# A graph layer on one core: squares turned on VectorE, sums sent through DRAM, products one group later

## The chip, the cores and the metric

The kernel runs on one core of a Trainium2 chip. The metric is the device time of one execution in microseconds (us). Before the change it is 2057.62 us, the median of three runs (2055.93 to 2058.0).

The core has a matrix engine (TensorE, in the profile PE; its loads of the stationary operand are PEld), VectorE (DVE), ScalarE (ACT), GpSimd (POOL) and SyncE (SP). Sixteen DMA engines move data between DRAM and the on-chip memories. Here POOL issues the indirect DMAs (gathers of rows by a list of indices) and SP the plain ones.

## The reference

`x` is 6250 x 512 (f32), `src` and `dst` are the ends of 100000 edges, sorted by `dst`. A graph convolution is applied twice, around a layer norm:

```
norm = -dinv[src] * dinv[dst]                    # dinv from the out-degrees
prop(h) = segment_sum(h[src] * norm, dst)        # for each node the sum of its neighbours' rows
conv(h; W0, W1, b) = h @ W0 + prop(h) @ W1 + b
h   = relu(layernorm(x))
h   = leaky(layernorm(conv(h; W1_0, W1_1, b1)) * gamma + beta)
out = x + conv(h; W2_0, W2_1, b2)
```

## The kernel before, in words

A prologue (up to some 110 us) makes the layer norm of x, the degrees, and a table in DRAM (`tab[0]`, rows of 512 values and one more for dinv). Then `usual_path` runs two layers with the same loop.

**Gathers and groups.** The edges lie in 782 chunks of 128. For each chunk POOL gathers the 128 source rows into one of 55 places in a ring (`gather_to`, line 444). Three chunks make a unit, which spans at most 32 target nodes, and four units a group: 66 groups a layer, 12 chunks in each but the first. `choose(g)` (VectorE) makes the 0/1 matrices `sel` of a group from the sorted targets, in layer 0 `scale` multiplies them by the gathered rows' dinv, and `sums(g)` (line 615) multiplies `sel` with the gathered rows: 24 matmul rows in the profile (two for each f32 matmul), four strips of 32 partitions. ACT takes the result out of PSUM to `agg[g]` (line 625). A place is free for a later gather when its matmul is done.

**Blocks.** The nodes lie in 49 blocks of 128 (46 whole ones on the usual way and three in `EARLY`, 46 to 48, which are handled partly ahead of time). A block's targets lie in two or three groups (`inside[i]`). When the last of them is summed, `turn` loads the block after next (`load`, `AHEAD` = 2), turns the block's own rows `h` with four TensorE transposes into `hT` (`own`, line 519, and an ACT eviction, line 521), and `place` moves the sums from their unit order to their nodes with one matmul a group (line 645, by the 0/1 matrices `there` of `spots`). ACT scales the result to `an` (line 698). `first_half` turns `an` with four transposes (line 705), VectorE copies them to `aT` (line 707), and the four products `hT @ W0` run. `second` adds the four products `aT @ W1` (all line 531) and calls `finish`: in layer 0 bias, layer norm, leaky relu, and two row stores, to the table of layer 1 (`tab[1]`, line 679) and to `h_tab` (line 684); in layer 1 bias, x (`load_x`) and the store of the output.

**Order.** TensorE, POOL and SP run in the order in which the program issues; VectorE and ACT are put in order by a scheduler that goes by its own cost model. An engine that waits holds up what stands behind it in its own queue. In the loop over groups, `turn` of a block stands before the group's `sums`, `first_half` behind them, and `second` before the following group's `place`, or with the next block's own turn. From the last 12 groups on (`JOIN`) `dense` runs both halves together behind the sums. At the end of layer 0 `gather_ahead` starts 18 chunks of layer 1 from the rows stored so far (those of blocks up to 46), and the rest wait for the stores of blocks 47 and 48. At the start SP loads h of blocks 0 and 1, and then the biases (`load_rest(4)`), which `widen` spreads over the partitions after the second group's sums; `look_up` scales the first raw chunks.

Of the kernel before, what the change touches and what calls it, by code (L numbers as in the profile page):

```python
# [8 lines left out]
F32 = mybir.dt.float32  # L9
# [10 lines left out]
P = 128  # L20
# [4 lines left out]
Q = 32  # L25
NQ = P // Q
# [7 lines left out]
JOIN = 12  # L34
# [8 lines left out]
def gnn_kernel(  # L43
# [61 lines left out]
    h_tab = dram.tile([N, D], F32, name="h_tab")  # L105

# [10 lines left out]
    first = const.tile([P, NQ * NS + 1], F32, name="first")  # L117
# [76 lines left out]
    def load_rest(k):  # L194
# [55 lines left out]
    with tc.tile_pool(name="turn", bufs=1) as wp, tc.tile_pool(  # L250
# [11 lines left out]
        nc.vector.tensor_copy(first, first_ps)  # L262
# [145 lines left out]
def usual_path(tc, have):  # L408
    nc = tc.nc
    (x, out, tab, h_tab, ndinv, sidx, dlx, iota_r, w_sb, W2_1, W2_0, w_late, ident, eps, ones, first, nodes_ps, node_of, minus,  # L410
     unsorted, dinv, sdinv, bias1, bias2, gam, bet, unseen, unit, N, E, D, NB, NC, NU, NS, KD, rows, places, R,
     load_rest, sc, pick, src_lo, src_hi, eidx, e_src, zero_row, p_id) = (
        have[n] for n in ("x out tab h_tab ndinv sidx dlx iota_r w_sb W2_1 W2_0 w_late ident eps ones first nodes_ps node_of "
# [13 lines left out]
    with ExitStack() as es:  # L427
# [5 lines left out]
        own_h, own_x, agg, placed, started, pre, late, theres = {}, {}, {}, {}, {}, {}, {}, {}  # L433
# [48 lines left out]
        def look_up(tag):  # L482
# [13 lines left out]
            both = pool.tile([P, D], F32, name="an")[:, : 8 * NB].rearrange("p (j k b) -> p j k b", j=4, k=2)  # L496
# [12 lines left out]

        def load(layer, i):  # L510
            if i not in EARLY:
                load_h(layer, i, "h", AHEAD)

        def own(layer, i):

            h, r = own_h.pop(i), rows[i]
            ps = psum.tile([P, KD, P], F32, name="hT_ps")
            for kc in range(KD):
                nc.tensor.transpose(ps[:, kc, :r], h[:r, kc * P : (kc + 1) * P], ident[:r, :r])  # L519
# [54 lines left out]
        def count_late(sel, chunk):  # L574
# [5 lines left out]
            for q in some:  # L580
                for b in range(LATE):
                    for k, t in enumerate(chunk[q]):
                        hot = pool.tile([P, P], F32, name="there", bufs=3)
# [4 lines left out]
            cnt = pool.tile([P, LATE, P], F32, name="cnt", bufs=1)  # L588
# [19 lines left out]
        def sums(layer, g, sel, chunk, cnt=None, of=(0, NQ)):  # L608
# [14 lines left out]
            if of[1] >= n:  # L623
                agg[g] = pool.tile([P, D], F32, name="agg", bufs=3)
                nc.scalar.activation(agg[g][: n * Q], ps[: n * Q], AF.Copy)  # L625

        def spots(i, some):

            r = rows[i]
            there = [pool.tile([P, P], F32, name="there", bufs=3) for _ in some]  # L630
            for t, g in zip(there, some):
                m = Q * (unit[g + 1] - unit[g])
                behind[1] = nc.vector.tensor_scalar(t[:m, :r], iota_r[:m, :r], node_of[:m, g : g + 1],  # L633
# [3 lines left out]
        def place(i, some):  # L637

            r = rows[i]
            if i not in placed:  # L640
                placed[i] = psum.tile([P, D], F32, name="an_ps", bufs=1)
            there = theres.pop(i) if i in theres else spots(i, some)
            for t, g in zip(there, some):
                m = Q * (unit[g + 1] - unit[g])
                nc.tensor.matmul(placed[i][:r], t[:m, :r], agg[g][:m, :], start=(g == inside[i][0]),  # L645
                                 stop=(g == inside[i][-1]))

# [38 lines left out]
        def turn(layer, i, left=()):  # L686

            r = rows[i]
# [4 lines left out]
            hT = None if i in EARLY else own(layer, i)  # L693
# [3 lines left out]
            an = pool.tile([P, D], F32, name="an")  # L697
            nc.scalar.activation(an[:r], placed.pop(i)[:r], AF.Copy, scale=ndinv[:r, i : i + 1])  # L698
            return hT, an

        def first_half(layer, i, hT, an, between=None):
            r = rows[i]
            ps = psum.tile([P, KD, P], F32, name="hT_ps")
# [4 lines left out]
            if between is not None:  # L708
                between()
            if i not in EARLY:  # L710
                started[i] = psum.tile([P, D], F32, name="u_ps")
                products(started[i], hT, w_late[:, 1] if layer else w_sb[1], rows[i], True, False)
            return aT

        def second(layer, i, aT):
            w1 = w_late[:, 0] if layer else w_sb[0]
# [4 lines left out]

        def dense(layer, i, hT, an, between=None):
            second(layer, i, first_half(layer, i, hT, an, between))

        def check():
# [19 lines left out]
            of = pool.tile([P, D], F32, name="xt")[0:1, :]  # L745
            nc.vector.tensor_sub(of[:, :NU], first[0:1, 1 : NU + 1], first[0:1, :NU])
# [49 lines left out]
        for layer in range(2):  # L796
# [4 lines left out]
            i, chosen, left = 0, {}, []  # L801
            for g in range(NS):
                gather_to(layer, STEP * unit[g] + R)
                if layer == 0 and g == NS // 2:
                    for k, w in enumerate((W2_1, W2_0)):
                        nc.sync.dma_start(w_late[:, k], w.rearrange("(k p) d -> p k d", p=P))
# [4 lines left out]
                due = []  # L811
                if g == NS - JOIN or inside[i].stop > g:
                    for k, aT in left:
                        second(layer, k, aT)
                    left = []
                while inside[i].stop <= g:
                    due.append((i, turn(layer, i, left)))
                    left = []
                    i += 1
                if g == NS - 2:  # L820
                    for k, (hT, an) in due:
                        dense(layer, k, hT, an)
# [4 lines left out]
                sel, chunk = chosen.pop(g) if g in chosen else choose(g)  # L827
                of = (NQ // 2, NQ) if g == NS - 1 else (0, NQ)
                if layer == 0 and g < NS - 1:
# [4 lines left out]
                if g < NS - 1:  # L834
                    chosen[g + 1] = choose(g + 1)
# [375 lines left out]
```

## Time and profile before

| what | us |
|---|---|
| median of three runs | 2057.62 |
| profiled execution, its own time | 2057.13 |
| its span | 2055.2 |
| PE busy | 1686.4 |
| POOL busy | 1513.0 |
| DVE busy | 701.1 |
| ACT busy | 406.6 |
| gathers in q0 | 415.98 MB, 67.5% of the DMA engines' time |
| plain DMAs in q1 | 110.12 MB, 14.8% |
| TensorE's mean granted clock | 0.912 |

Busy time of PE overlaps and its ends are modelled. A row of the profile's fifth part names line, engine, operation, output and input, shape and count; behind the bar stand the busy time, the mean of one in ns, and the idle time of the engine just before such instructions, with what ended most of it. "issue" there is time for which the profile shows no wait. A row of the order of time has start, length, engine, line, operation, count, and in brackets the idle time before it and what ended it. A row of the stretches has its bounds, its length, busy time and count by engine, the clock, the share of the DMA engines and GB/s.

### The profile page before, as it was taken

The page shows a single profiled execution, that of the slowest core. Times are in us where ns is not written, and L with a number is a line of the kernel's source. Part 1 is how long each engine was busy: PE and PEld are TensorE (multiplying, and loading weights), DVE is VectorE, ACT ScalarE, POOL GpSimd, SP SyncE. Part 2 cuts the span into 40 slices and gives each one's busy share as a digit, 9 for nine tenths or more (in the row PEclk, how much of TensorE's full clock was granted, in tenths as well). Part 3 has the DMA queues.
Part 4 walks back from the last instruction along what each step waited for, and adds up shares of the span by engine and source line. Part 5 has one row for each costly group of instructions (what it writes and reads, how often), then busy time and mean ns, then how long its engine had stood idle before and what let it go on. Part 6 is the DMA issues. An engine that isn't in the chain of part 4 may idle for free.

```text
span 2055.2 us, 19878 instructions
## 1 busy us (share of the span) xinstructions
PE 1686.4 (82%) x6814; PEld 675.0 (33%) x6814; DVE 701.1 (34%) x1501; ACT 406.6 (20%) x740; POOL 1513.0 (74%) x1578
## 2 busy tenths in 40 slices
PE   5569997788777778777899888888888888898987
PEld 4444432233222223333333223233322223333332
DVE  7955442334434333543452211122121212121221
ACT  8766221112211111221120100110110111010110
POOL 5757777777777777777767777777777777777774
PEclk9769998899898889889999989999999999999999
DMA  9978888888898888888877887887788888778875
GB/s 360 360 258 237 274 265 255 247 262 263 255 298 249 255 248 263 262 254 255 256 240 236 253 249 245 251 255 246 247 252 250 246 252 255 243 249 255 270 237 158
DMA packets 189415, 527.47 MB, mean 257 GB/s; under 512 B 34550, under 2 KB 36112, under 8 KB 189304
## 3 DMA queue, kind: packets, MB, share of 16 engines
q0 software_dynamic: 125120, 415.98, 67.5%
q1 hardware_dynamic: 64184, 110.12, 14.8%
q8 instruction: 56, 0.92, 0.2%
q14 instruction: 55, 0.45, 0.1%
HBM read 474.31 MB, written 51.66 MB: 256 GB/s over the span
## 4 chain that ended last, share of the span: by engine, by line
PE 47%; DMA 25%; POOL 11%; issue 9%; DVE 5%; ACT 1%; SPq 1%; DVEq 0%; POOLq 0%; ACTq 0%
DMA places<-tab,sidx 19%; PE u_ps L531 19%; PE ps L615 13%; POOL places L444 11%; PE an_ps L645 9%; DMA places<-tab,lidx 5%; PE hT_ps L519 2%; PE hT_ps L705 2%; DVE lo L340 1%; DVE hi L340 1%; SPq L508 1%; PE hT_ps L491 1%; PE hT_ps L586 0%; DVE sel L604 0%; DVE st L665 0%
## 5 line engine op out<-in xcount | busy, mean ns | idle before, releaser
L444 POOL DMA_INDIRECT places<-tab,sidx x1212 | 1148.8, 948 | 386.5 <-issue 271.3
L615 PE MATMUL ps<-places,sel 128*32 128x512 f32 x3128 | 523.6, 680 | 155.8 <-DMA places<-tab,sidx 90.2
L645 PE MATMUL an_ps<-agg,there 128*128 128x512 f32 (+1 forms) x580 | 284.5, 623 | 101.8 <-ACT agg L625 96.8
L444 POOL DMA_INDIRECT places<-tab,lidx x270 | 255.5, 946 | 82.2 <-issue 62.1
L615 PEld LDWEIGHTS ps<-places,sel 128*32 128x32 f32 x3128 | 105.0, 119 | 542.7 <-issue 195.9
L570 DVE TENSOR_TENSOR sel<-dlx,nodes_ps 128x384 f32<-128x384 f32 (+3 forms) x134 | 72.2, 540 | 423.8 <-PE ps L615 423.4
L625 ACT ACTIVATE agg<-ps 128x512 f32<-128x512 f32 (+1 forms) x132 | 78.3, 594 | 573.1 <-PE ps L615 552.7
L531 PE MATMUL u_ps<-w,hT 128*128 128x512 f32 (+1 forms) x392 | 178.5, 599 | 13.0 <-ACT hT L521 13.0
L645 PEld LDWEIGHTS an_ps<-agg,there 128*128 128x128 f32 (+1 forms) x580 | 110.6, 200 | 228.8 <-ACT agg L625 115.0
L531 PE MATMUL u_ps<-places,hT 128*128 128x512 f32 (+1 forms) x392 | 179.1, 600 | 2.2 <-ACT hT L521 2.2
L531 PE MATMUL u_ps<-w,aT 128*128 128x512 f32 (+1 forms) x392 | 176.9, 594 | 1.7 <-DVE aT L707 1.7
L531 PE MATMUL u_ps<-places,aT 128*128 128x512 f32 (+1 forms) x392 | 176.6, 593 | 1.5 <-DVE aT L707 1.5
L604 DVE TENSOR_TENSOR sel<-sel,places 128x384 f32<-128x384 f32 (+11 forms) x73 | 35.1, 484 | 375.5 <-DMA places<-tab,sidx 370.0
L656 DVE TENSOR_TENSOR u_ps<-u_ps,bias 128x512 f32<-128x512 f32 x46 | 32.2, 699 | 288.5 <-PE u_ps L531 288.5
L521 ACT ACTIVATE hT<-hT_ps 128x512 f32<-128x512 f32 (+1 forms) x98 | 58.2, 594 | 284.3 <-PE hT_ps L519 283.7
L633 DVE TENSOR_SCALAR there<-iota_r,node_of 128x128 f32<-128x128 f32 (+1 forms) x290 | 86.9, 303 | 66.4 <-PE an_ps L645 63.5
L698 ACT ACTIVATE an<-an_ps,ndinv 128x512 f32<-128x512 f32 (+1 forms) x98 | 67.1, 684 | 206.7 <-PE an_ps L645 206.5
L236 POOL DMA_INDIRECT places<-in_x_dram,sidx x55 | 79.1, 1438 | 36.8 <-issue 9.1
L668 ACT ACTIVATE sd<-mv,eps 128x1 f32<-128x1 f32 (+1 forms) x49 | 14.4, 294 | 455.4 <-DVE mv L666 455.4
L531 PEld LDWEIGHTS u_ps<-w,aT 128*128 128x128 f32 (+1 forms) x392 | 71.8, 190 | 84.3 <-issue 78.3
L531 PEld LDWEIGHTS u_ps<-places,aT 128*128 128x128 f32 (+1 forms) x392 | 72.1, 190 | 83.1 <-issue 80.4
L531 PEld LDWEIGHTS u_ps<-w,hT 128*128 128x128 f32 (+1 forms) x392 | 71.3, 192 | 85.1 <-issue 71.5
(166 smaller groups left out, 1272.9 us busy)
## 6 DMA issues: line engine op xcount, KB each, us to landing
places<-tab,sidx POOLq DMA_INDIRECT x1212, 3.9
h_tab<-g SPq DMA_DIRECT2D x48, 256.0 KB
xt<-in_x_dram SPq DMA_DIRECT2D x48, 256.0 KB
out_dram<-t SPq DMA_DIRECT2D x48, 256.0 KB
tab<-t SPq DMA_DIRECT2D x47, 256.0 KB
h<-tab SPq DMA_DIRECT2D x46, 256.0 KB
h<-h_tab SPq DMA_DIRECT2D x46, 256.0 KB
tab<-places SPq DMA_DIRECT2D x22, 528.0 KB
```

Source lines behind the costliest of these rows:

```text
L236: nc.gpsimd.indirect_dma_start(out=places[:, t, :D], out_offset=None, in_=x, in_offset=bass.IndirectOffsetOnAxis(ap=sidx[:, t : t + 1], ax ...
L340: nc.vector.tensor_tensor(t, s[:, g * 2 * GJ : (g + 1) * 2 * GJ].rearrange("p (j s) -> p j s", s=2)[:, :, None, :] .to_broadcast([EP, GJ, ...
L444: nc.gpsimd.indirect_dma_start(out=places[:, t % R, :] if own_scale else zr(layer, t), out_offset=None, in_=x if layer == 0 and t < RAW el ...
L519: nc.tensor.transpose(ps[:, kc, :r], h[:r, kc * P : (kc + 1) * P], ident[:r, :r])
L521: nc.scalar.activation(hT[:, :, :r], ps[:, :, :r], AF.Copy)
L531: nc.tensor.matmul(u_ps[:r], hT[:, kc, :r], w[:, kc, :], start=(start and kc == 0), stop=(stop and kc == KD - 1))
L570: nc.vector.tensor_tensor(sel[:, q : q + k, :w, :], of, node[:, q : q + k, None, :].to_broadcast([P, k, w, Q]), op=OP.is_equal)
L615: nc.tensor.matmul(ps[q * Q : (q + 1) * Q, :], sel[:, q, s, :], zr(layer, chunk[q][s]), start=(s == 0), stop=(s == len(chunk[q]) - 1 and ( ...
L625: nc.scalar.activation(agg[g][: n * Q], ps[: n * Q], AF.Copy)
L633: behind[1] = nc.vector.tensor_scalar(t[:m, :r], iota_r[:m, :r], node_of[:m, g : g + 1], -(1.0 + i * P), op0=OP.subtract, op1=OP.is_equal)
L645: nc.tensor.matmul(placed[i][:r], t[:m, :r], agg[g][:m, :], start=(g == inside[i][0]), stop=(g == inside[i][-1]))
L698: nc.scalar.activation(an[:r], placed.pop(i)[:r], AF.Copy, scale=ndinv[:r, i : i + 1])
```

## The change

1. `own` no longer uses TensorE. A block of h is loaded as four strips of 32 partitions: strip c holds, for its partition i, the 128 columns from 128c on of rows i, 32+i, 64+i and 96+i (`load_squares`: four DMAs, each with 128 runs of 512 bytes). One VectorE transpose (`turn_squares`), which turns squares of 32 x 32 in place in the layout, gives `hT`, with feature 4p+k on partition p. The weights are loaded in that order of rows, `(p k) d`.
2. The scaled sums go from PSUM by ACT to `an`, from there by a DMA on ACT's queue to DRAM (`a_tab`), and are read back as squares (`sh`) by four DMAs on SP; one VectorE transpose makes `aT`. The three blocks of `EARLY` keep TensorE's transposes, with strided columns.
3. Before the last 12 groups (`FLUSH`) the order in a group is: sums(g); both products of the block that was pending; place, scaling, store, loads and turns of the block that is complete with group g-1, which is then pending. So all eight matmuls of a block run a group later, together.
4. `choose` runs one group further ahead, `scale` of the next group stands before `sums(g)`, `spots` makes its up to three matrices in one tile, ahead of the sums; `first` is copied only where the check uses it; some tiles share buffers. In the last 12 groups `turn`, sums and `dense` keep their order.

```diff
-                nc.sync.dma_start(t, w.rearrange("(k p) d -> p k d", p=P))
+                nc.sync.dma_start(t, w.rearrange("(p k) d -> p k d", p=P))
...
+        def load_squares(to, of, i):
+            for c in range(P // S):
+                nc.sync.dma_start(to[c * S : (c + 1) * S],
+                                  of[i * P : (i + 1) * P, c * P : (c + 1) * P].rearrange("(g i) f -> i g f", i=S))
+
+        def turn_squares(to, of):
+            return nc.vector.transpose(to.rearrange("p k (g i) -> p g k i", i=S), of.rearrange("p g (j k) -> p g k j", k=KD))
+
         def load(layer, i):
             if i not in EARLY:
-                load_h(layer, i, "h", AHEAD)
+                own_h[i] = pool.tile([P, P // S, P], F32, name="h", bufs=AHEAD)
+                load_squares(own_h[i], h_tab if layer else tab[0], i)
 
         def own(layer, i):
             h, r = own_h.pop(i), rows[i]
+            if i not in EARLY:
+                hT = pool.tile([P, KD, P], F32, name="hT", bufs=1)
+                turn_squares(hT, h)
+                return hT
...
-        def place(i, some):
+        def place(i, some, there=None):
...
+        def scaled_rows(i):
...
+            nc.scalar.activation(an, placed.pop(i), AF.Copy, scale=ndinv[:, i : i + 1])
+            nc.scalar.dma_start(a_tab[layer_of[0]][i * P : (i + 1) * P, :], an)
+            sh = pool.tile([P, P // S, P], F32, name="sh", bufs=1)
+            load_squares(sh, a_tab[layer_of[0]], i)
+            return sh
...
+        def turned(i, an):
+            if i not in EARLY:
+                aT = pool.tile([P, KD, P], F32, name="aT", bufs=1)
+                behind[2] = turn_squares(aT, an)
+                return aT
...
-        def first_half(layer, i, hT, an, between=None):
...
-        def second(layer, i, aT):
...
+        def dense(layer, i, hT, aT):
+            w0, w1 = (w_late[:, 1], w_late[:, 0]) if layer else (w_sb[1], w_sb[0])
             if i not in EARLY:
                 started[i] = psum.tile([P, D], F32, name="u_ps")
+                products(started[i], hT, w0, rows[i], True, False)
             whole = i not in started
             u_ps = psum.tile([P, D], F32, name="u_ps") if whole else started.pop(i)
             products(u_ps, aT, w1, rows[i], whole, True)
             finish(layer, i, u_ps)
...
-                if g == NS - JOIN or inside[i].stop > g:
-                    for k, aT in left:
-                        second(layer, k, aT)
-                    left = []
+                due, new = [], []
+                if g == NS - FLUSH:
+                    for k, hT, aT in pending:
+                        dense(layer, k, hT, aT)
+                    pending = []
                 while inside[i].stop <= g:
-                    due.append((i, turn(layer, i, left)))
-                    left = []
+                    if g >= NS - FLUSH:
+                        due.append((i, turn(layer, i)))
+                    else:
+                        new.append(i)
                     i += 1
...
-                sel, chunk = chosen.pop(g) if g in chosen else choose(g)
+                sel, chunk = chosen.pop(g)
+                if g < NS - 1:
+                    chosen[g + 1] = choose(g + 1)
+                theres = [spots(k, inside[k]) for k in new]
...
+                if layer == 0 and g < NS - FLUSH:
+                    scaled = scale(*chosen[g + 1])
                 sums(layer, g, sel, chunk, count_late(sel, chunk) if layer == 1 else None, of)
...
-                if g < NS - JOIN - 1 and inside[i].stop <= g + 1:
-                    theres[i] = spots(i, inside[i])
+                if g < NS - FLUSH:
+                    with ExitStack() as order:
+                        if layer == 0 and scaled is not None:
+                            order.enter_context(tc.issue_after(scaled.ins))
+                        for k, hT, aT in pending:
+                            dense(layer, k, hT, aT)
+                        pending = []
+                        for k, there in zip(new, theres):
+                            place(k, inside[k], there)
+                            sh = scaled_rows(k)
+                            pending.append((k, own_part(layer, k), turned(k, sh)))
                 for k, (hT, an) in due:
-                    if g < NS - JOIN:
-                        left.append((k, first_half(layer, k, hT, an)))
-                    else:
-                        dense(layer, k, hT, an)
+                    dense(layer, k, hT, turned(k, an))
```

More of the change, by code (lines that the diff above doesn't have):

```diff
@@ L105, in gnn_kernel @@
     h_tab = dram.tile([N, D], F32, name="h_tab")
+    a_tab = [dram.tile([N, D], F32, name=f"a_tab{i}") for i in range(2)]
     ident = const.tile([P, P], F32, name="ident")
@@ L432, in usual_path @@
         behind, behind_rows, summed = {}, {}, {}
-        own_h, own_x, agg, placed, started, pre, late, theres = {}, {}, {}, {}, {}, {}, {}, {}
+        layer_of = [0]
+        own_h, own_x, agg, placed, started, pre, late = {}, {}, {}, {}, {}, {}, {}
         SHIFTED = D - D % P
@@ L684, in finish, with own_part @@
                 nc.sync.dma_start(h_tab[i * P + lo : i * P + hi, :], g[lo:hi])
-        def turn(layer, i, left=()):
-            r = rows[i]
+        def own_part(layer, i):
             if layer == 1 and i not in EARLY:
@@ L800, in usual_path @@
                     load(layer, i)
[L801 removed]
+            i, chosen, pending = 0, {}, []
+            layer_of[0] = layer
             for g in range(NS):
```

95 lines of the change are left out of this document (50 added, 45 removed).

## The prediction

> **What bounds the kernel now.** I read the page first. It suggests TensorE, with 82% busy and 47% of the chain, so I checked that against POOL.
>
> ```profile
> span 2055.2 us, 19878 instructions
> PE 1686.4 (82%) x6814; PEld 675.0 (33%) x6814; DVE 701.1 (34%) x1501; ACT 406.6 (20%) x740; POOL 1513.0 (74%) x1578
> L444 POOL DMA_INDIRECT places<-tab,sidx x1212 | 1148.8, 948 | 386.5 <-issue 271.3
> q1 hardware_dynamic: 64184, 110.12, 14.8%
> ```
>
> A gather is 0.948 us busy and has some 0.30 us of "issue" before it: 1.25 us each, which the 74% does not count. The stretches of line 444 alone (length, POOL busy, clock, DMA share, GB/s) show that nothing comes between:
>
> ```profile
> 300.00:350.00 50.00, 37.93 (x40) 0.85 0.83 242
> 650.00:700.00 50.00, 37.82 (x41) 0.93 0.86 264
> 1200.00:1250.00 50.00, 37.82 (x40) 0.91 0.81 247
> 1700.00:1750.00 50.00, 37.83 (x40) 0.91 0.82 254
> ```
>
> 37.8 us is 40 gathers of 0.945, and 40 x 1.25 = 50: POOL issues without a break, in both layers. Its order of time has only these holes (start, length, idle before):
>
> ```profile
> 153.52 0.97 POOL L444 DMA_INDIRECT places<-tab,sidx  x1 [12.15 <-PE ps L615]
> 1052.23 0.94 POOL L454 DMA_INDIRECT places<-tab,eidx  x1 [5.57 <-DMA tab<-t]
> 1077.56 0.99 POOL L444 DMA_INDIRECT places<-tab,sidx  x1 [2.80 <-DMA tab<-pre]
> 2031.74 0.94 POOL L444 DMA_INDIRECT places<-tab,lidx  x1 [0.30 <-issue]
> ```
>
> From 153.5 to 2032.7 there are 1494 gathers: 1494 x 1.25 = 1867 us of the 1879; the two holes in the middle are 7.8 us beyond the usual 0.3. TensorE in this time is paced by the gathers: the list of waits has 282 us of its loads and 125 us of its matmuls in L615 waiting for places. A faster TensorE gains nothing where POOL has no hole. What can change is the start, the layer change, the tail, or the pace of the gathers itself.
>
> **The change part by part.** All is reckoned on the profiled execution, 2057.1 us (span 2055.2 and 1.9 around it); the median is 2057.6.
>
> *TensorE.* For 46 blocks in each of two layers go 4 turns of h and 4 of the sums, 0.44 + 0.59 us a block in the chain: 92 x 1.03 = 95 us. The wait for agg before place (96.8 us in all) goes too before the last 12 groups, since place now follows the next group's sums. Worth 0: POOL's 15.0 us a group (12 x 1.25) hide it. Without that cover it would be 190 us.
>
> *ACT and VectorE.* ACT loses 92 evictions hT of 0.595 (55 us), and issues 92 stores behind an; ACT is 20% busy, so 0. VectorE loses 92 copies aT of 0.687 and gains 184 turns of 128x512. No row shows such a turn. The nearest are the 128x512 f32 operations at 0.69 to 0.76; a cast of 128x896 took 0.62, so below is some 0.4, above I allow four times the copy, 2.8. I take 0.69: net +64 us on an engine 34% busy, off the path. Removing the copy first (0.43 us at 16 us) lies beside loads: 0.
>
> *The way by DRAM.* After an (0.69) ACT issues the store, SP waits for it, issues four loads, VectorE turns. Landings: the store tab<-t issued at 1049.46 released POOL at 1052.2 (2.8 us), that of tab<-pre at 1072.7 took 4.5 beside gathers, the bias loads of 130.4 to 136.4 some 5.5. I take 4.5 for each way, since gathers run beside both: 0.3 + 4.5 + four issues of 0.35 + 4.5 + 0.7 = 11.4 us, between 8.0 (2.8 each) and 13.4 (5.5 each). Products a group later hide it under sums(g+1) 2.7 and the own products 3.4, but place(k+1) stands behind the products of k on TensorE. So block to block: 0.7 + 11.4 + 3.4 + 2.6 = 18.1 us. Some 46 blocks finish in 63 groups, three in four; the fourth group adds its sums: (3 x 18.1 + 2.7) / 4 = 14.3 us a group against POOL's 15.0. It fits, with 5% to spare, and the 55 places let TensorE lag by over a group: cost 0. The Trainium skill, "DMA: Bandwidth & Descriptors", section "Anatomy of one DMA", puts some 2 us of fixed time on every DMA, most of it the write's receipt. By an estimate from it the way is 6.4 us and the loop 10.5 a group, comfortably hidden; the landings of 2.8 to 5.5 here say otherwise.
>
> *What waits behind it.* The turn of the sums waits on VectorE for its squares; behind it stand finish(k), the next spots and the choose of two groups on. sums(g+1) needs none of these, since sel of g+1 is made a group ahead: 0 up to a wait of 15 us. In layer 0 scale of g+1 now stands ahead of sums(g) and waits for the gathers of g+1, with finish(k-1) and the turns behind it; finish is some 5.7 us of VectorE and ACT rows, so a turn can come 6 us after the gathers land, where TensorE, too, has only just got its next sums. 0, and the reason why layer 0 is the first to slip if the way is longer. The one tile for three there waits for the last place (VectorE's wait of 63.5 us for it stays) and has a group's time: 0. count_late has fewer buffers at the start of layer 1, where POOL is 55 gathers, 69 us, ahead: 0. The weights' other row order moves the same bytes once: 0.
>
> *SP.* Ten issues a block in layer 0 where three were, at 0.32 to 0.51: some 3 us in 20, and a wait for the store. Behind it stand load_x and h(i+2), needed a group or two later: 0. Only at the start does SP's order show:
>
> ```profile
> 114.20 16.12 SPq L508 DMA_DIRECT2D h<-tab  x2
> 130.37 0.59 SPq L204 DMA_DIRECT2D bias<-in_L_gnn_b_dram  x2
> 136.46 2.07 PE L793 MATMUL u_ps<-bias,ident 1*128 1x512 f32 x2 [12.11 <-DMA bias<-in_L_gnn_b_dram]
> ```
>
> The biases stand behind h(0) and h(1). widen waits for them, look_up and sums(2) for widen, and POOL for sums(2) (the 12.15 us). Eight loads in place of two: 6 x 0.40 = +2.4 us, straight on the path (0 to +4).
>
> *The DMA engines.* All of q1 is 14.8% of 2055 = 304 us for 110.12 MB: 0.72 us per 256 KB. Rows of 512 B: the 384 KB id loads at 3 to 4 us ran at 153 GB/s with a share of 0.64, so 240 GB/s full, 1.09 us per 256 KB:
>
> ```profile
> 3.00:3.50 0.50, 0.00 (x0) 0.00 (x0) 0.00 (x0) 0.00 (x0) 0.50 (x1) 1.00 0.62 150
> 3.50:4.00 0.50, 0.00 (x0) 0.00 (x0) 0.00 (x0) 0.00 (x0) 0.50 (x3) 1.00 0.66 157
> ```
>
> Below is the 2 KB price, 0.72; above, 512 B cost as much as 2 KB each, 2.9. I take 1.09, the only row of that size. A block adds a store 0.72, the sums' squares 1.09, and 0.37 on h: 2.2 us. At 2.4 blocks per 50 us that is +0.105 of share: 0.85 to 0.96 in layer 0, 0.81 to 0.92 in layer 1. Under 1, so POOL keeps its pace: 0.
>
> *Layer change.* Blocks 44, 45, 46 finish in consecutive groups; gather_ahead waits for the row store of 46. The chain now:
>
> ```profile
> 1023.36 2.58 PE an_ps L645 x6
> 1025.93 2.71 PE ps L615 x24
> 1028.64 0.59 PE hT_ps L705 x4
> 1029.23 6.87 PE u_ps L531 x16
> 1036.10 2.59 PE an_ps L645 x6
> ```
>
> Here a block's way by DRAM has only sums and own products over it (6.1 of 11.4 us). place(44) ends at 1011.1, its last matmuls having waited 5 us for agg. From there: an and the way to 1023.2, products 1026.6, place(45) 1029.2, again 12.1 + 3.4 + 2.6, so place(46) ends at 1047.3 in place of 1038.7, +8.6. If agg comes in time, place(44) ends some 6.6 us sooner and place(46) at 1040.7, +2. I take +5; with the shortest way, 8.0, it would be 1033.9, which is -4.8.
>
> *Tail.* The same there in layer 1, where TensorE waits for gathers until 2008.5 and the way of 45 mostly fits into it; 46 to 48 keep TensorE's turns: +1 (-1 to +4).
>
> Sum: 2057.1 + 2.4 + 5 + 1 = 2065.5, own range 2056 to 2074.
>
> **The rivals.** Slow is forecast, so "Faster" ends on the other side. 0.2%, 4 us, is about what a measurement here can tell from no change: 2053.5 to 2061.7.
>
> *The loop becomes the bound.* If the way by DRAM takes over 12.4 us the loop exceeds 15.0 a group, places fill and POOL waits for sums. At 13.5 us: (3 x 20.2 + 2.7) / 4 = 15.8, 0.83 x 54 groups x 2 = +89, some 2154 with the rest; in layer 0 alone, 2110. It starts there too if a turn takes 1.7 us or more in place of 0.69. For it: 5.5 us landings, VectorE's order (a finish of some 6 us, or a scale that waits for gathers, ahead of the turn). Against: the average landing. 0.17.
>
> *The DMA engines fill.* From 1.56 us per 256 KB of 512 B rows layer 0 reaches share 1. At 2.1 (a block adds twice the row's price, 4.2): 1.05 and 1.01, so +45 on the 890 us of gathers of layer 0 and +10 on the 950 of layer 1: 2120. For: shares already at 0.85; against: 240 GB/s in the only row. 0.10.
>
> *VectorE holds up the gathers.* Gathers that start inside VectorE's one-hot operation take 2.53 us, not 0.95:
>
> ```profile
> 27.15 1.78 DVE L340 TENSOR_TENSOR hi<-s_hi,iota_g 125x3136 bf16<-125x3136 bf16 x1
> 27.22 2.54 POOL L236 DMA_INDIRECT places<-in_x_dram,sidx  x1 [0.30 <-issue]
> ```
>
> Such a gather ends some 0.8 us after the operation. If a turn of 0.69 does this too, 0.55/1.25 of 184 gathers lose 0.28 each: +22, 2088. For: a sel times places of 0.5 us stretched a gather at 230.63 to 1.18. Against: the 0.3 us one-source operations L633 leave gathers at 0.95. The Trainium skill, "DMA: Bandwidth & Descriptors", section "SWDGE vs HWDGE vs iDMA", says VectorE's 2-port mode locks GpSimd out of the descriptor rings it writes; whether a turn uses that mode no row here shows. 0.12.
>
> *Faster.* agg comes in time and the way takes 8.0 us: place(46) is 4.8 us sooner, the first middle hole all but closes (-4.8), the second, 2.5 us, goes with it, and the start costs its +2.4: 2052.2. It decides from some 6 us of holes regained, as a store of 46 landed by 1047. For: agg is 5 us late only because ACT's sd stands ahead of it and waits for VectorE. Against: the landings beside gathers. 0.12.
>
> **How the numbers follow.** The forecast has 0.49; 0.18 of it lies within 0.2%, at the cheap ends of its three terms, and 0.31 above. The slow rivals have 0.39, the fast one 0.12. So faster 0.12, same 0.18, slower 0.70. The range leaves out some 0.08 of the fast side and the upper half of the loop and DMA cases, 0.12: 2053 to 2115.
>
> **What would show it.** Right: line 444 still at 40 per 50 us; a first hole of some 14.5 us; shares near 0.96 and 0.92; no hT_ps rows but for three blocks; turns near 0.69 us. Wrong: fewer than 40 gathers per 50 us, with releaser PE ps (loop) or at share 1 (DMA), gathers much over 0.95 us (VectorE), or the holes at the layer change gone.

## The result, and the profile after

The changed kernel took **2371.48 us** (median of four, 2367.81 to 2383.77) against 2056.77 for the kernel before on the same chip: a ratio of 1.154, 95% interval 1.151 to 1.158. The forecast was 2065.5 in a range of 2053 to 2115: slower it is, but by 314 us and not by 9.

The profiled execution took 2383.77 us, the longest of the four; its span is 2381.8. The page of the changed kernel, the lines that answer to those shown of before:

```profile
span 2381.8 us, 19523 instructions
...
PE 1667.9 (70%) x6078; PEld 649.8 (27%) x6078; DVE 841.3 (35%) x1593; ACT 355.6 (15%) x648; POOL 1511.8 (63%) x1578
...
PE u_ps L547 23%; DMA sh<-a_tab 18%; DMA a_tab<-an 12%; PE an_ps L662 9%; PE ps L632 6%; SPq L514 4%; DVE aT L518 4%; DMA places<-tab,sidx 2%; POOL places L445 2%; ACT an L673 2%; DVE hi L340 1%; DMA h<-tab 1%; DVE lo L340 1%; DMA h_tab<-g 1%; PE hT_ps L492 1%
...
L445 POOL DMA_INDIRECT places<-tab,sidx x1212 | 1149.9, 949 | 571.6 <-issue 290.8
```

A gather still takes 0.949 us, and the same number are made; what grew is POOL's idle time before them, 386.5 to 571.6 us. The chain that ended last (its shares by line are above) hardly holds a gather any more: the products of L547, and the way of the placed sums to DRAM and back (a_tab, sh, L514, aT), are some 60% of it.

The stretches of the gathers' line in the changed kernel (length, POOL busy, clock, DMA share, GB/s), two of layer 0 and one of layer 1:

```profile
300.00:350.00 50.00, 32.87 (x36) 0.80 0.85 244
650.00:700.00 50.00, 33.57 (x36) 0.83 0.87 256
...
1700.00:1750.00 50.00, 37.81 (x41) 0.86 0.91 272
```

In layer 0 POOL makes 36 gathers in 50 us where it made 40. In layer 1 it still makes 40 or 41 until about 1800 us. POOL's order of time shows the holes; the bracket has the idle time and what ended it:

```profile
158.10 0.98 POOL L445 DMA_INDIRECT places<-tab,sidx  x1 [17.13 <-PE ps L632]
...
339.78 0.95 POOL L445 DMA_INDIRECT places<-tab,sidx  x1 [6.78 <-PE ps L632]
...
1275.88 0.94 POOL L455 DMA_INDIRECT places<-tab,eidx  x1 [51.05 <-DMA tab<-t]
...
2312.61 0.95 POOL L445 DMA_INDIRECT places<-tab,lidx  x1 [0.30 <-issue]
```

The holes of layer 0 end when TensorE's sums (ps, L632) free a place: the 55 places are full, and POOL waits for TensorE. From this view the whole difference of the two spans can be laid out, 2381.8 - 2055.2 = 326.6 us: the start +4.6 (158.1 for 153.5), layer 0's gathers +173.6, the hole at the layer change +45.5 (51.05 for 5.57), layer 1's gathers +57.2, and the stretch behind the last gather +45.7 (2381.8 - 2313.6 = 68.2, for 22.5).

The list of waits of the changed kernel (total us, times, longest) names whom TensorE waits for:

```profile
PE u_ps L547 <- DVE aT L518: 604.8, 92, 10.7
...
DVE aT L518 <- DMA sh<-a_tab: 397.5, 90, 10.1
...
POOL places L445 <- PE ps L632: 274.0, 97, 17.1
```

Ninety-two blocks take the way by DRAM, and before the products of each of them TensorE stands for 6.6 us on average. One block of the chain, in order of time (start, us, what):

```profile
507.64 0.69 ACT an L673
508.35 6.15 DMA a_tab<-an
514.51 0.32 SPq L514
...
515.83 4.79 DMA sh<-a_tab
520.74 1.09 DVE aT L518
521.87 5.22 PE u_ps L547 x8
527.09 2.58 PE an_ps L662 x6
529.66 2.71 PE ps L632 x24
```

The block's an starts at 507.64, and the next block can be placed only behind its products on TensorE; the next an starts at 529.70. That is 22.0 us from block to block, where the gathers for a block take 20.5 (945 us for 63 groups of 15.0, over 46 blocks). With one group in four that finishes no block it is (3 x 22.0 + 2.7) / 4 = 17.2 us a group, against POOL's 15.0. That is the pace seen in layer 0: in the 400 us from 200 on the changed kernel made 278 gathers, 1.439 us each, and 12 x 1.439 = 17.3. Layer 1 starts with empty places, which give POOL a lead of 55 x 1.25 = 69 us, and its blocks are shorter: the 17 from 1409.4 to 1790.9 take 22.4 us on average, with the groups that finish no block, and 46 x 22.4 / 63 = 16.4 us a group. So POOL keeps its pace until it first waits for TensorE at 1834, and only then slows: from 1806 to 2200 it makes 291 gathers, 12 x 1.354 = 16.2 us a group.

This is the mechanism of the rival "The loop becomes the bound". What had to be tested is whether it is the loop at all, what in it is longer than forecast, and why the layer change and the tail lost 91 us more.

### The profile page after: what moved, and what is told of

The parts are those of the page before. It is cut to its first block, busy times and chain, and to the rows that moved or that the text cites. A ratio compares the mean times of both kernels' runs of the same rounds, so it can differ in the third digit from the quotient of the medians.

```text
span 2381.8 us, 19523 instructions
## 1 busy us (share of the span) xinstructions
PE 1667.9 (70%) x6078; PEld 649.8 (27%) x6078; DVE 841.3 (35%) x1593; ACT 355.6 (15%) x648; POOL 1511.8 (63%) x1578
## 4 chain that ended last, share of the span: by engine, by line
PE 41%; DMA 34%; DVE 9%; issue 5%; SPq 4%; ACT 3%; POOL 2%; DVEq 0%; POOLq 0%; ACTq 0%
PE u_ps L547 23%; DMA sh<-a_tab 18%; DMA a_tab<-an 12%; PE an_ps L662 9%; PE ps L632 6%; SPq L514 4%; DVE aT L518 4%; DMA places<-tab,sidx 2%; POOL places L445 2%; ACT an L673 2%; DVE hi L340 1%; DMA h<-tab 1%; DVE lo L340 1%; DMA h_tab<-g 1%; PE hT_ps L492 1%
## 5 line engine op out<-in xcount | busy, mean ns | idle before, releaser
L445 POOL DMA_INDIRECT places<-tab,sidx x1212 | 1149.9, 949 | 571.6 <-issue 290.8
L547 PE MATMUL u_ps<-w,aT 128*128 128x512 f32 (+1 forms) x392 | 281.7, 885 | 347.2 <-DVE aT L518 345.7
L547 PE MATMUL u_ps<-places,aT 128*128 128x512 f32 (+1 forms) x392 | 281.7, 885 | 260.6 <-DVE aT L518 259.1
L632 PE MATMUL ps<-places,sel 128*32 128x512 f32 x3128 | 388.0, 606 | 6.9 <-DMA places<-tab,sidx 6.9
L547 PEld LDWEIGHTS u_ps<-w,aT 128*128 128x128 f32 (+1 forms) x392 | 109.0, 293 | 516.6 <-DVE aT L518 383.8
L518 DVE STREAM_TRANSPOSE aT<-sh 128x512 f32<-128x512 f32 x92 | 99.4, 1080 | 397.5 <-DMA sh<-a_tab 397.5
L547 PEld LDWEIGHTS u_ps<-places,aT 128*128 128x128 f32 (+1 forms) x392 | 109.0, 293 | 430.3 <-DVE aT L518 297.2
L547 PE MATMUL u_ps<-places,hT 128*128 128x512 f32 (+1 forms) x392 | 181.5, 606 | 2.0 <-ACT hT L537 2.0
L547 PE MATMUL u_ps<-w,hT 128*128 128x512 f32 (+1 forms) x392 | 181.2, 605 | 2.0 <-ACT hT L537 2.0
L632 PEld LDWEIGHTS ps<-places,sel 128*32 128x32 f32 x3128 | 92.4, 110 | 273.3 <-issue 227.9
L518 DVE STREAM_TRANSPOSE hT<-h 128x512 f32<-128x512 f32 x92 | 99.3, 1080 | 175.6 <-PE u_ps L547 150.7
L673 ACT ACTIVATE an<-an_ps,ndinv 128x512 f32<-128x512 f32 x92 | 63.2, 687 | 577.5 <-PE an_ps L662 577.4
L687 DVE TENSOR_TENSOR u_ps<-u_ps,bias 128x512 f32<-128x512 f32 x46 | 32.2, 700 | 274.9 <-PE u_ps L547 274.9
L693 DVE TENSOR_TENSOR u_ps<-u_ps,bias 128x512 f32<-128x512 f32 x46 | 32.2, 700 | 270.8 <-PE u_ps L547 270.8
L547 PEld LDWEIGHTS u_ps<-places,hT 128*128 128x128 f32 (+1 forms) x392 | 70.5, 190 | 112.3 <-issue 109.7
```

The source lines that it names most:

```text
L445: nc.gpsimd.indirect_dma_start(out=places[:, t % R, :] if own_scale else zr(layer, t), out_offset=None, in_=x if layer == 0 and t < RAW el ...
L518: return nc.vector.transpose(to.rearrange("p k (g i) -> p g k i", i=S), of.rearrange("p g (j k) -> p g k j", k=KD))
L547: nc.tensor.matmul(u_ps[:r], hT[:, kc, :r], w[:, kc, :], start=(start and kc == 0), stop=(stop and kc == KD - 1))
L632: nc.tensor.matmul(ps[q * Q : (q + 1) * Q, :], sel[:, q, s, :], zr(layer, chunk[q][s]), start=(s == 0), stop=(s == len(chunk[q]) - 1 and ( ...
L673: nc.scalar.activation(an, placed.pop(i), AF.Copy, scale=ndinv[:, i : i + 1])
L687: nc.vector.tensor_add(v, v, bias2[:r])
```

## Experiments

The theory: the way by DRAM stands between two blocks' places on TensorE, and its length sets the time. The rivals: the added transfers, VectorE's turns, the own rows' new path, or products run a group later cost the time by themselves.

**Taking the way out of the loop.** In e_place_first a block is placed, and its way started, ahead of the products that wait for the way of the block before:

```
+ placed_now = []
+ for k, there in zip(new, theres):
+     place(k, inside[k], there); placed_now.append((k, scaled_rows(k)))
  for k, hT, aT in pending: dense(layer, k, hT, aT)
  pending = []
- for k, there in zip(new, theres):
-     place(k, inside[k], there); sh = scaled_rows(k)
+ for k, sh in placed_now:
      pending.append((k, own_part(layer, k), turned(k, sh)))
```

> The changed kernel with one thing in another order: before the last 12 groups, place and the way by DRAM of the block that has just been completed stand ahead of the products of the pending block, no longer behind them. The same work, transfers and turns. Theory of the loop (place of k+1 stands behind the products of k, which wait for the way of k: some 22 us from block to block, (3 x 22 + 2.7) / 4 = 17 us a group against POOL's 15): the loop is cut, line 445 is back at 40 gathers per 50 us in both layers, and what is left is the start (+5), and the last 12 groups, which still wait for the way: 2065 to 2090 us. If the DMA engines are full, it stays above 2200, with the share near 1. If VectorE's turns hold up the gathers, it stays above 2300, since all 184 turns are there.

Measured: 2186.32 us, a ratio of 1.062 (1.060 to 1.064) to the kernel before: 185 us of the 314 are gone, not all, and the 2065 to 2090 expected are missed by some 100. Its stretches (columns as above):

```profile
300.00:350.00 50.00, 37.84 (x40) 0.89 0.97 280
...
1000.00:1050.00 50.00, 33.87 (x37) 0.84 0.82 238
1100.00:1150.00 50.00, 0.00 (x0) 0.93 0.25 80
```

In most of layer 0 POOL is back at its old pace, with the same bytes and turns, and even with the DMA engines at a share of 0.97. The steady loop was the right cause for that part. The way itself did not get shorter: from the end of an to the turn it took 14.0 us on average, where it took 11.2 in the changed kernel. Once it stands outside the loop its length no longer counts. What is left is at the ends of the layers: its hole ahead of layer 1 is 49.24 us, nearly what it was. Its chain there (start, us, what):

```profile
989.13 0.70 ACT an L673
989.85 3.45 DMA a_tab<-an
...
994.66 4.42 DMA sh<-a_tab
999.20 1.09 DVE aT L518
1000.34 5.92 PE u_ps L547 x8
1006.26 2.83 PE ps L632 x24
...
1010.34 3.70 PE u_ps L547 x8
1014.04 2.59 PE an_ps L662 x6
1016.65 0.70 ACT an L673
```

In the last 12 groups (FLUSH) a block's products aren't put off, and so the whole way stands in the chain: 27.5 us from an to an in this pair. The eight blocks that finish there in layer 0 took 194.8 us together (from the an at 930.84 to the one at 1125.64), 24.3 each; in the kernel before the same eight took 147.1.

**Doubling a known piece of the loop.** e_evict_twice scales the placed sums twice, one more 0.7 us ahead of each store:

```
+ nc.scalar.activation(an, placed[i], AF.Copy, scale=ndinv[:, i : i + 1])
  nc.scalar.activation(an, placed.pop(i), AF.Copy, scale=ndinv[:, i : i + 1])
  nc.scalar.dma_start(a_tab[...], an)
```

> The changed kernel, with ACT's scaling of the placed sums done twice, one after the other, ahead of the store: 0.69 us more on each block's way, no transfer more. Theory of the loop: each of the some 80 blocks at which TensorE is behind the gathers is 0.69 us later, so +50 to +60 us, some 2425. If the DMA engines or the gathers bind, the 0.69 us lie on an engine busy 15% of the time and it is within 10 us of the changed kernel.

Measured: 2421.55 us (one run), 50 over the changed kernel's median. ACT is only 17% busy there, so this price is that of a place in the chain: 92 times 0.7 is 64 us, and most of it shows.

**The parts without the sums' way.** e_sums_pe keeps the own rows' turn by VectorE and the products a group later, and turns the sums on TensorE as before; e_own_pe is the other half, own rows by TensorE and sums by way of DRAM; e_traffic is the kernel before with the sums' store and their four reads added, whose data nobody uses (two small buffers make room for it).

```
e_sums_pe  - nc.scalar.dma_start(a_tab[...], an); load_squares(sh, a_tab[...], i); turn_squares(aT, sh)
           + nc.tensor.transpose(ps[:, kc, :r], an[:r, kc * P : (kc + 1) * P], ident[:r, :r])  # x4, and the copy to aT
e_own_pe   - load_squares(own_h[i], ...); turn_squares(hT, h)
           + load_h(layer, i, "h", AHEAD)       # and TensorE's four turns with ACT's copy
e_traffic  + nc.scalar.dma_start(a_tab[layer][...], an)
           + nc.sync.dma_start(sh[c * 32 : (c + 1) * 32], a_tab[layer][...])   # x4
```

> One part of the change taken back: the placed sums are turned by four TensorE transposes and a VectorE copy, as before; the own rows come as squares with one VectorE turn, and the products still run a group later. Theory of the loop: the way is 0.7 + 0.7 + 0.7 us, the loop some 12 us, POOL keeps 40 per 50 us: 2057 to 2070 us. If the squares of the own rows (512-byte rows) or their turns cost by themselves, half of the loss or more stays: above 2200.

> The other part taken back: the own rows are loaded in whole rows and turned by TensorE and ACT as before; the sums still go by DRAM and one VectorE turn. Theory of the loop: the way is as long as it was, and four TensorE transposes of 0.44 us a block come in beside it: 2350 to 2400 us, no gain. If the cost comes from 512-byte rows in all, half of the squares are gone and a good part of the 315 us with them: below 2250.

> The kernel before, with the way by DRAM added and used by nobody: each placed sum is also stored to DRAM from ACT's queue and read back as four squares on SP's; TensorE turns it as before. Theory of the loop: no one waits for it, so 2057 to 2066 us, with a share of the DMA engines some 0.08 higher (from 0.85 and 0.81). If the traffic itself is the cost, it is above 2150.

Measured: e_sums_pe 2063.98 us, ratio 1.0029 (1.0019 to 1.0039). e_own_pe 2340.28 (one run; the kernel before took 2055.49 beside it). e_traffic 2057.49, ratio 0.9995 (0.9986 to 1.0005). So the added transfers cost nothing, the own rows by VectorE and the products a group later together cost 6 us, and the sums' way alone, without the own rows' turn, brings back 285 of the 315 us. Why e_own_pe came some 10 us under its expectation was not followed up.

**Another way of the same kind.** e_sbuf moves the sums within the on-chip memory with 16 transfers, half of them issued by SP and half by ACT, and leaves the store to DRAM out of it:

```
- nc.scalar.dma_start(a_tab[...], an); load_squares(sh, a_tab[...], i)
+ for c in range(4):
+     for g in range(4):
+         (nc.sync if c % 2 else nc.scalar).dma_start(sh[c*S:(c+1)*S, g], an[g*S:(g+1)*S, c*P:(c+1)*P])
```

> The changed kernel with the way made shorter: no store to DRAM, the sixteen squares of the scaled sums go straight from one on-chip tile to the other, eight DMAs from SP's queue and eight from ACT's. One landing in place of two. Theory of the loop: 0.7 + 0.3 + 8 x 0.35 + 4.5 + 1.1 + 5.2 products + 2.6 place = 17 us, (3 x 17 + 2.7) / 4 = 13.4 a group, under POOL's 15: 2070 to 2130 us, most of the loss gone although the order is the same. If it is the number of DMAs that costs, it is slower than the changed kernel.

Measured: 2440.44 us, ratio 1.187 (1.185 to 1.189). The expectation failed. The chain says why; one block of it:

```profile
616.20 0.70 ACT an L673
...
618.99 4.82 DMA sh<-an
623.83 0.51 SPq L677
...
626.28 0.59 SPq L677
626.91 3.37 DMA sh<-an
...
630.46 1.09 DVE aT L518
```

The way did not become shorter: ACT's issues lie between its other work, SP's issues take 0.5 to 0.6 us each and stand behind a landing, and from the end of an to the turn it is 13.6 us, where the changed kernel's block above took 12.4. The turns are at 606.02 and 630.46, 24.4 us apart. Over layer 0 (32 blocks) it is 24.8 us a block, for 23.7 in the changed kernel. So a longer loop gave a longer time, which fits the theory; the figure for its length was mine, and wrong. In layer 1 it was not longer (21.7 for 22.4), and little time was lost there: of the 59 us between the two spans 56 are there by the first an of layer 1 (1390.6 for 1334.4).

**The ends of the layers.** e_late_pe is the changed kernel with the sums of the blocks of the last 12 groups turned on TensorE, the steady loop left as it is; e_pf_late_pe is that and e_place_first together.

```
- if i in EARLY:          # in scaled_rows: no store
+ if i in EARLY or inside[i].stop >= NS - FLUSH:
...
- if i not in EARLY:      # in turned: else by TensorE
+ if i not in EARLY and inside[i].stop < NS - FLUSH:
```

> The changed kernel, with the sums of the blocks that finish in the last 12 groups of a layer (those whose last group is 50 or later) turned by TensorE, as three blocks already are; the loop of the first 51 groups, with its 22 us from block to block, stays. If the loop and the last groups are two separate losses, the loop's share stays (some +174 us in layer 0's gathers, less the 12 groups' part, and some +57 in layer 1) and the layer change (+45) and the tail (+46) go back to some +5 to +20 each: 2371 - 60 to 100, some 2270 to 2310. If the layer change and the tail are only what TensorE's lag from the loop leaves behind, the time stays over 2340.

> Place ahead of the waiting products (which alone gave 2186) and, in addition, the sums of the blocks of the last 12 groups turned by TensorE. If the 129 us that were left over are the last 12 groups of the two layers, where a block still goes through the way by DRAM before the next can be placed, it comes to within 20 us of the kernel before: 2060 to 2080, and the wait before the first gathers of layer 1 goes from 49 us to under 12. If something else of the change holds it up there (one tile for three spots, fewer buffers in the counting at the start of layer 1, VectorE's order), it stays over 2120.

Measured: e_late_pe 2260.58 us (one run), e_pf_late_pe 2075.27, ratio 1.0096 (1.0079 to 1.0113). The two losses are separate and add up: place first alone saves 185, late blocks on TensorE alone 111, both 296. The number of stores, 92 in the changed kernel and 76 here, says how many blocks the second part is: 8 in each layer. (The expectation says that they finish from group 50 on; by the edit they are the blocks whose last group is 53 or later.) In e_place_first these eight took 194.8 us in layer 0 and 192.9 in layer 1, in e_pf_late_pe 122.3 and 150.3: the 115 us between them are about the 111 gained. In e_late_pe the hole ahead of layer 1 shrank from 51.05 to 24.51 us, but its stretch behind the last gather is still 46.7: so the expectation failed for the tail, while the time came 10 us under its range. POOL still waits for TensorE's sums until 2102 there, so TensorE enters the tail 55 places behind, the lag of the steady loop. With the loop alone mended, in e_place_first, the stretch is 64.7, since the late blocks still go by DRAM. With both mended, in e_pf_late_pe, it is 22.8, against 22.5 before. The time of e_pf_late_pe is inside its range; the wait ahead of layer 1, expected under 12 us, is not. Its holes are these:

```profile
156.80 0.97 POOL L445 DMA_INDIRECT places<-tab,sidx  x1 [15.73 <-PE ps L632]
...
1068.55 0.94 POOL L455 DMA_INDIRECT places<-tab,eidx  x1 [16.84 <-DMA tab<-t]
...
1094.65 0.94 POOL L445 DMA_INDIRECT places<-tab,sidx  x1 [3.88 <-DMA tab<-pre]
```

Its span is 17.3 us over that of before: 3.3 at the start (156.8 for 153.5) and 12.4 at the layer change (16.84 for 5.57 and 3.88 for 2.80) make up nearly all of it. At the layer change TensorE still comes late: the an of its first late block starts 41 us later than in the kernel before (932.7 for 891.6), and the an behind the eighth 16 us later. Where that lag comes from was not tried.

**What makes the products slow.** In the chain above the products of the sums took 5.22 us, where the kernel before took 3.44 (half of the 6.87 for sixteen pieces in the prediction's chain). TensorE's granted clock around them, changed kernel (length, busy, clock, DMA share, GB/s), and its order of time:

```profile
521.00:527.00 6.00, 5.13 (x9) 0.67 0.93 274
527.00:531.00 4.00, 4.00 (x23) 1.00 0.77 227
```

```profile
521.87 5.22 PE L547 MATMUL u_ps<-w,aT 128*128 128x512 f32 x8 [7.98 <-DVE aT L518]
```

The clock is low behind the wait of some 8 us and back at 1.00 some 5 us later. In e_warm TensorE makes the own rows' products three times over, the first two results being overwritten: a block's eight pieces become 24, and the sixteen that are added are work for nothing.

```
+ for k in range(2 if inside[i].stop < NS - FLUSH else 0):
+     products(started[i], hT, w0, rows[i], True, True)
  products(started[i], hT, w0, rows[i], True, False)
```

> The changed kernel, with the four products of a block's own rows made three times over (the first two results are overwritten) for the blocks before the last 12 groups, so that TensorE works for 6.9 us more (8 matmuls, two pieces each, at 0.43) where it now waits some 8 us for the turned sums. The loop is 22 us; the products of the sums take 5.2 to 6.4 us of it where they took 3.4 before, in stretches with a granted clock of 0.67, and the same instructions have a median of 1061 ns and a minimum of 592. If it is the wait that lowers the clock, more work in the wait makes the kernel faster: products back to some 3.5 to 4 us, loop 22 to some 20, over some 80 blocks, 2230 to 2320. If the products are slow for another reason, the added work changes nothing or delays: 2365 to 2420.

Measured: 2284.55 us (one run): 87 us faster than the changed kernel, with 355 us more of TensorE's work (2023.4 us busy for 1667.9). Its order of time and its clock in the same place, and then the pieces of the sums' products by tile (shortest, median and longest in ns) in the changed kernel and in this one:

```profile
519.87 3.70 PE L547 MATMUL u_ps<-w,aT 128*128 128x512 f32 x8 [0.39 <-DVE aT L518]
```

```profile
516.00:523.00 7.00, 6.61 (x17) 1.00 1.08 284
```

```profile
L547 PE MATMUL u_ps<-w,aT x392: 592/1061/1224, 187.6 to 1290.8; 128*128 128x512 f32 x192, 128*106 128x512 f32 x4
```

```profile
L547 PE MATMUL u_ps<-w,aT x392: 592/592/1223, 188.6 to 1225.3; 128*128 128x512 f32 x192, 128*106 128x512 f32 x4
```

With the wait filled the clock stays at 1.00, the median piece is 592 ns in place of 1061, and the block is 19.9 us (503.69 to 523.57, from place to place) in place of 22.0. The Trainium skill, "TensorE: Matmul & The Clock Gate", section "HAM oscillation — how this bites in real kernels", says that a gap of over some 3.4 us throttles TensorE's clock to half, so that each burst behind a wait for data starts cold; both kernels agree, with a wait of 7.98 us and a clock of 0.67 behind it, and a wait of 0.39 us and 1.00.

**The bound before, tested by itself.** e_bias_first is the kernel before, with the biases loaded ahead of the first two blocks' own rows; e_pf_late_bias is e_pf_late_pe with that edit.

```
  load_rest(3)
+ load_rest(4)
  for i in range(AHEAD):
      load(0, i)
- load_rest(4)
```

> The kernel before with SP's loads of the four bias rows ahead of those of h(0) and h(1), nothing else. If POOL's stream of gathers is all that sets the time, as the prediction had it, the hole of 12 us at 153 us closes to some 2 to 4 us and the time falls by as much: 2047 to 2050 us, ratio 0.995 to 0.9965. If TensorE or the DMA engines bind, nothing changes.

> The same with the biases loaded ahead of the first two blocks' own rows, which gave the kernel before 12 to 14 us. The start's wait is POOL's own, so it should give the same here: 12 to 16 us under the run without it, some 2048 to 2066, against 2043.6 of the kernel before with that edit.

Measured: e_bias_first 2043.59 us, ratio 0.9943 (0.9930 to 0.9957). It is the fastest of all the kernels here, some 3 us under its range, and it confirms what bounded the kernel before: the hole of 12.15 us in POOL's order closes, and 12 us go. In e_pf_late_bias the same edit gives nothing: 2074.87, for 2075.27 without. That expectation failed, and VectorE's order of time shows what is late in its place:

```profile
140.66 1.08 DVE L518 STREAM_TRANSPOSE hT<-h 128x512 f32<-128x512 f32 x1 [14.38 <-DMA h<-tab]
141.67 0.65 DVE L827 COPY bias<-u_ps 128x512 f32<-128x512 f32 x1
```

The turn of the first block's own rows stands on VectorE ahead of the copy of the biases, and waits 14 us for their load. In e_bias_first the same copy is at 126.51.

## Why the prediction was wrong, point by point

**What bounds the kernel before: right.** POOL's stream of gathers, 1.25 us each without a hole. e_bias_first gained from POOL's hole and nothing else, and e_pf_late_pe, with TensorE 45 us less busy than before (1641.6 for 1686.4), gained nothing.

**The way by DRAM: the step that failed.** It said that the way takes 11.4 us, the loop 18.1 and a group 14.3, which "fits, with 5% to spare". The runs showed 22.0 and 17.2 in layer 0. Of the 3.9 us two are the way and two the products behind it:

| term of the loop, us | taken | block at 507.64 |
|---|---|---|
| an | 0.7 | 0.7 |
| store lands, with its issue | 4.8 | 6.15 |
| four issues | 1.4 | 1.3 |
| squares land | 4.5 | 4.8 |
| turn, and the step from it to TensorE | 0.7 | 1.2 |
| products of the sums | 3.4 | 5.2 |
| place | 2.6 | 2.6 |

The landings were taken at 4.5 from rows of 2.8 to 5.5, and the way measured some 13.4 to 13.5, the upper bound that the step itself gave. With 5% to spare a sum with such bounds should not have been called a cost of 0: the threshold of 12.4 lay inside them. The products were taken at 3.4 from a kernel in which TensorE hardly stood still ahead of them; the step had TensorE wait, and did not ask what the wait does to what comes behind it. By e_warm that term is worth 87 us, even with the added work beside it.

Of the two the products weigh more. On average the eight pieces behind a turn lasted 5.7 us in the changed kernel's order of time, in both layers, 3.6 in the kernel before and 4.1 in e_warm. The way, from the end of an to the turn, was 12.2 us on average in layer 0 (38 blocks), but 10.7 in layer 1, just what the step had (0.3 + 4.5 + 1.4 + 4.5): and layer 1 was over POOL's pace all the same, at 16.4 us a group. With 5.2 for the products in its own sum the step would have had room for a way of 10.6 us, less than the 11.4 that it forecast. The kernel before showed the effect already. In its chain, behind a wait of TensorE of 12.14 us for agg, at a clock of 0.50 (527 to 532 us), the sums of a group took 4.44 us in place of 2.71:

```profile
527.57 2.07 PE an_ps L645 x2
529.64 4.44 PE ps L615 x24
```

**The rival "The loop becomes the bound": the right mechanism, too cheap.** It had the releaser (PE ps), the place (layer 0 first) and, with 13.5 us, the way. Its price of 2154 lacked the slow products (15.8 us a group in place of 17.2) and the ends of the layers.

**Layer change +5 and tail +1: far too small.** Measured were +45.5 and +45.7. The step reckoned with blocks 44 and 45 and a TensorE on time. In fact 8 blocks a layer run in the last 12 groups with the whole way in the chain, 24.3 us each in e_place_first, and that is 111 us by e_pf_late_pe against e_place_first; and TensorE came 55 places late. With both mended the layer change still costs some 12 us and the tail 0.3.

**The start, +2.4: half the size, and half of the path.** The first hole moved by 4.6 us (3.3 in e_pf_late_pe). SP's order is on the path, as the step had it: the eight loads of h kept SP for 20.80 us where two had kept it for 16.12, +4.7 in place of +2.4, and the matmuls that spread the biases waited for their load 16.9 us, by this line of the waits, where it was 12.11:

```profile
PE u_ps L826 <- DMA bias<-in_L_gnn_b_dram: 16.9, 1, 16.9
```

e_pf_late_bias shows a second thing behind it, which the step left out: with SP's order mended, VectorE's turn of the first own rows ahead of the copy of the biases holds the start as long.

**TensorE's saving and the added issues, 0: right** as far as e_traffic and e_pf_late_pe can tell. **The turn, 0.69:** it took 1.08, inside the bounds; off the loop it cost nothing (e_sums_pe has 92 turns of own rows, and its 6 us hold the start and the layer change too).

**The DMA engines, 0: right.** e_traffic is at 0.9995, and e_place_first made 40 gathers in 50 us at a share of 0.97, close to the 0.96 that was worked out. **VectorE holds up the gathers: it does not.** There are 184 turns, and a gather's mean stays at 949 ns; the 135 gathers of the changed kernel that start inside a turn take 948 on average and 960 at most. **Faster:** it needed a way of 8.0 us; beside the gathers no block of the chains shown here had one.

## What to carry to other kernels

A transfer taken out and back in "a step later" is hidden only if nothing that the next step needs stands behind its consumer in the same in-order engine: follow the engine's order from one block to the next, add up that loop, and compare it with the bound's pace using the slow end of each landing. Where the loop makes TensorE wait, price what follows the wait at the lower clock. And look for a flush or drain part that runs without the pipelining: there the full length is paid, once per block.

## What the runs showed of the hardware that I had not expected

- More work made the kernel faster: with 355 us more on TensorE, and nothing else changed, 2371 became 2285, because the wait of 8 us that it filled had cost the next products nearly half their speed (1061 to 592 ns).
- Landings of 256 KB were longer beside the gathers than without them, in the block shown over twice as long. There a store took 6.15 and the read 4.79; behind the last gather, in the lines of the same chain below, 2.18 and 1.94. In the hole ahead of layer 1, where POOL stood still, two reads took 1.92 and 1.97. The Trainium skill, "DMA: Bandwidth & Descriptors", section "Anatomy of one DMA", puts about 2 us of fixed cost on a DMA that GpSimd issues. These were issued by ACT and SP: their whole landings without the gathers are near that figure, and in the block beside the gathers they took over twice as much. That the gathers are the cause was not tried by itself.
- Moving the 256 KB in 16 pieces within the on-chip memory was no faster than to DRAM and back: an issue took 0.5 to 0.6 us, and in the block shown 13.6 us passed from an to the turn, for 12.4.
- VectorE's turn of 128x512 f32 took 1.08 us, where its copy of the same size from TensorE's sums had taken 0.69.
- POOL kept its pace of 40 gathers in 50 us with the DMA engines at a share of 0.97.

The chain of the changed kernel behind its last gather (start, us, what), for the second point of this list:

```profile
2331.21 2.18 DMA a_tab<-an
...
2334.76 1.94 DMA sh<-a_tab
```
